# Differential attention with routed experts on one core: experts' steps spread by TensorE columns, and the two attentions of half the head groups added on VectorE

## The chip, the cores and the metric

The kernel runs on one core of a Trainium2 chip. The core has a matrix engine (TensorE, PE in the profile, with its weight loads as PEld), VectorE (DVE), ScalarE (ACT), GpSimd (POOL) and SyncE (SP), which only issues transfers. Each engine works through its own queue in order and waits on semaphores. The metric is the device time of one execution in microseconds; lower is better.

## The reference

The input x is (8, 512, 128): eight sequences of 512 tokens. All data are 32-bit floats.

```python
s1, s2 = q·k1 * SCALE, q·k2 * SCALE          # 16 heads of 8, causal
attn = softmax(s1) - sigmoid(lambda) * softmax(s2)
attn = attn / maximum(sum(abs(attn)), 1e-6)
x = layernorm(x + (attn @ v) @ Wo.T)
xn = layernorm(x) * gamma + beta             # router and experts
probs = softmax(xn @ router.T / 1.5); w, idx = top_k(probs, 2)
y = sum over the two chosen of w * (silu(xn @ W1[e]) @ W2[e])     # 8 experts, 128 -> 512 -> 128
out = layernorm(x + y)
```

## The kernel before

**Units, slots, rounds.** The attention goes through a sequence in 16 row blocks of Q = 32 queries, each a `Unit` with L = 32, 64, ..., 512 keys. The four heads of a group times 32 queries fill the 128 partitions; there are NG = 4 groups. Four units make a token block of 128 tokens (32 blocks in all, n = 0 to 31). A unit with L up to 256 is early: two slots, each with two groups and both softmaxes. A later unit has four slots, each with two groups and one softmax. One call of `round_of` (line 1062) issues one round; a sequence has 16 early and 32 late rounds.

**Order in a round.** `round_of` writes out the order for every engine by hand. For the current slot (`now`), with the next one as `ahead`: the multiplication by V of units that are through (`times_v`, line 469) and, after every fourth unit, `reciprocals`; the scores of `ahead` on TensorE (line 343, with the causal mask added by line 352) into one of two PSUM buffers of the pool `ps_s`; on ScalarE the copies of the last round's transposes (`evacuate`, lines 457 and 459); the row maxima of `now` on VectorE (lines 365 and 373); the transposes of pieces combined in the round before (line 437); then `combine`; then the exponentials of `now` on ScalarE (line 383), which also add up their rows. After that come one task each of `misc` (projections, the end of a block) and `routing`, one of `moves` or `gathers`, and up to two experts' steps.

**Two softmaxes.** `exps` leaves both exponentials of a group unscaled in `et`, at index 0 and 1. With c2 = lambda * sum0 / sum1 (`ratios`), the difference is et0 - c2 * et1, up to a factor per row. `combine` has VectorE take the row sum of max(c2 * et1, et0) (line 409, into `junk`, the sum into `big`), from which `reciprocals` gets the sum of magnitudes, as 2 * big - (1 + lambda) * sum0. GpSimd multiplies et1 by -c2 (line 419). TensorE transposes both and adds them in PSUM: two matmuls per group and 128 keys.

**Experts.** Tokens are routed in chunks: four sparse ones of 6, 9, 9 and 6 blocks and a last dense one of 2. When a chunk's last block is through, `route_tasks` computes the choice, `send` scatters the rows to DRAM by expert with indirect transfers on GpSimd's queue (line 751), and `go` puts the experts' steps into a queue. A sparse chunk of nb blocks has 2nb + 7 tiles of 128 rows. `hidden` computes a tile's hidden layer (line 874) in a PSUM buffer of the pool `ps_m` (two buffers); `turn` transposes a gathered tile, computes the output of an earlier one (lines 845 and 854) and issues the loads of a later tile's rows and weights (256 KB twice) on SP's queue. `gathers` fetch the results back (line 899) and add them (line 909).

**When a step goes.** `times` estimates each round by its columns, and `go` sets `pace`, experts' steps per unit of that time, up to the next chunk's estimated arrival. Each round adds its time times `pace` to `due`, and a step goes for each whole `due`. After the attention `round_of` runs without `now`, and `due` grows by 2 per round.

Of the kernel before, what the change touches and what calls it, by code (L numbers as in the profile page):

```python
# [9 lines left out]
F32 = mybir.dt.float32  # L10
# [3 lines left out]
AF = mybir.ActivationFunctionType  # L14
ALU = mybir.AluOpType
# [5 lines left out]
def kernel(  # L21
# [16 lines left out]
    P = 128  # L38
# [95 lines left out]
    with ExitStack() as actx:  # L134
# [29 lines left out]
        won = aw.tile([P, D], F32, name="won")  # L164
        wo_sb = aw.tile([P, 4, D], F32, name="wo_sb")
        slam = aw.tile([P, NG], F32, name="slam")
        slam1 = aw.tile([P, NG], F32, name="slam1")
        hm = aw.tile([P, 4], F32, name="hm")
        hms = aw.tile([P, 4], F32, name="hms")
# [1 line left out]
        i4 = aw.tile([P, 4, Q], BF16, name="i4")  # L171
        mk = aw.tile([P, Q], BF16, name="mk")
        junk = aw.tile([P, T], F32, name="junk")

        xts = {}

# [47 lines left out]
            )  # L224
        nc.scalar.activation(slam, slam, AF.Sigmoid)
        nc.vector.tensor_scalar(slam1, slam, 1.0, None, ALU.add)
        for h in range(4):
            nc.vector.tensor_scalar_mul(wo_sb[:, h, :], won, hm[:, h : h + 1])

# [86 lines left out]
        class Unit:  # L316


            def __init__(self, b, j, blk):
# [11 lines left out]
                self.et = ep.tile([P, NG, 2, T], F32, tag="et", name=f"et_{b}_{j}")  # L331
                self.aT = self.c2 = None

            def scores(self, slot):
                gp, s = slot
                qb, kT, _ = qkv[self.b]
                L, j = self.L, self.j
                sc = ps_s.tile([P, 2, T], F32, tag="sc", name=f"sc_{self.b}_{j}_{gp}_{s}")
                for si in range(2) if s is None else (s,):
                    lo = 0 if s is not None else si * (T // 2)  # L340
                    for gi in range(2):
                        r = slice(32 * (2 * gp + gi), 32 * (2 * gp + gi) + 32)
                        nc.tensor.matmul(  # L343
                            sc[:, gi, lo : lo + L],
                            lhsT=qb[r, j].rearrange("p h q -> p (h q)"),
                            rhs=kT[r, si, :L],
                            start=True,
                            stop=False,
                        )
                    for gi in range(2):  # L350
                        r = slice(32 * (2 * gp + gi), 32 * (2 * gp + gi) + 32)
                        nc.tensor.matmul(  # L352
                            sc[:, gi, lo + L - Q : lo + L],
                            lhsT=i4[r].rearrange("p h q -> p (h q)"),
                            rhs=mk[r],
                            start=False,
                            stop=True,
                        )
                return sc
# [31 lines left out]
            def ratios(self):  # L391

                sums, jj = self.blk["sums"], self.jj
                c1 = sp.tile([P, NG], F32, tag="c1", name=f"c1_{self.b}_{self.j}")
                nc.vector.tensor_mul(c1, sums[:, 0, jj, :], slam)
                self.c2 = sp.tile([P, NG], F32, tag="c2", name=f"c2_{self.b}_{self.j}")
                r2 = sp.tile([P, NG], F32, tag="r2", name=f"r2_{self.b}_{self.j}")
                nc.vector.reciprocal(r2, sums[:, 1, jj, :])
                nc.vector.tensor_mul(self.c2, c1, r2)

            def combine(self, piece):

                if self.c2 is None:
                    self.ratios()
                L = self.L
                for g in piece:
                    nc.vector.scalar_tensor_tensor(  # L409
                        junk[:, :L],  # L410
                        self.et[:, g, 1, :L],
                        self.c2[:, g : g + 1],
                        self.et[:, g, 0, :L],
                        ALU.mult,
                        ALU.max,
                        accum_out=self.blk["big"][:, self.jj, g : g + 1],
                    )
                for g in piece:
                    nc.gpsimd.tensor_scalar(  # L419
                        self.et[:, g, 1, :L],  # L420
                        self.et[:, g, 1, :L],
                        self.c2[:, g : g + 1],
                        -1.0,
                        ALU.mult,
                        ALU.mult,
                    )

            def widths(self):
                return [min(P, self.L - P * kb) for kb in range(self.n)]

            def transposes(self, piece):

                pt = ps_t.tile([P, 4, P], F32, tag="pt", name=f"pt_{self.b}_{self.j}_{piece[0]}")
                for x_, g in enumerate(piece):
                    for kb, kw in enumerate(self.widths()):
                        for k in range(2):
                            nc.tensor.matmul(  # L437
                                pt[:kw, x_ * self.n + kb, :],
                                lhsT=self.et[:, g, k, kb * P : kb * P + kw],
                                rhs=ident,  # L440
                                is_transpose=True,
                                start=(k == 0),
                                stop=(k == 1),
                            )
                return pt

# [30 lines left out]
        def block_tasks(b, i, blk):  # L477
# [7 lines left out]
            def reciprocals():  # L485
                s["oraw"] = op.tile([P, JT, P], F32, tag="oraw", name=f"oraw_{n}")
                nc.scalar.copy(s["oraw"], blk["po"])

                dg = bp.tile([P, JT, NG], F32, tag="dg", name=f"dg_{n}")
                nc.vector.tensor_mul(  # L490
                    dg, blk["sums"][:, 0], slam1.unsqueeze(1).to_broadcast([P, JT, NG])
                )
                nc.vector.scalar_tensor_tensor(dg, blk["big"], 2.0, dg, ALU.mult, ALU.subtract)
                nc.vector.scalar_tensor_tensor(
                    dg, blk["sums"][:, 0], 1e-6, dg, ALU.mult, ALU.max
                )
                rd = bp.tile([P, JT, NG], F32, tag="rd", name=f"rd_{n}")
                nc.vector.reciprocal(rd, dg)
                s["rexp"] = op.tile([P, JT, NG, 32], F32, tag="rexp", name=f"rexp_{n}")
                nc.gpsimd.tensor_copy(s["rexp"], rd.unsqueeze(3).to_broadcast([P, JT, NG, 32]))  # L500
# [78 lines left out]
        def route_tasks(ch):  # L579
# [176 lines left out]
                )  # L756

            def go():
                nonlocal pace
                first, *others = sparse_tasks(ch) if ch.sparse else dense_tasks(ch)  # L760

                experts.insert(max(0, len(experts) - 4), first)
                experts.extend(others)

                k = chunks.index(ch) + 1
                later = [at for at in arrival[k:] if now_at + 3 < at < time_all]
                pace = len(experts) / max((later + [time_all])[0] - now_at, 3.0)

            def together(*steps):
                def both():  # L770
# [45 lines left out]
        def silu_doubled(pz, dst, name, pool=hp, tag="th"):  # L816
# [4 lines left out]
                lambda: nc.vector.scalar_tensor_tensor(dst, th, 1.0, pz, ALU.add, ALU.mult)  # L821
            )

        def sparse_tasks(ch):
            n0, nt, nb = ch.n0, ch.nt, ch.nb
            w, xg, xgT, hT = {}, {}, {}, {}
# [42 lines left out]
                    load(t + 2)  # L869

            def hidden(t):
                pz = ps_m.tile([P, NF, P], F32, tag="pm", name=f"pz_{n0}_{t}")
                for f in range(NF):
                    nc.tensor.matmul(  # L874
                        pz[:, f, :],
# [160 lines left out]
                if n == ch.n0 + ch.nb - 1:  # L1036
                    misc.append(lambda: routing.extend(route_tasks(ch)))

        def time_of(width):

            return (0.5 + width / 1024) / 1.5

        def times():

            at, now, ends = [], 0.0, {}
            for n in range(NB):
                for j in range(n % NT * JT, (n % NT + 1) * JT):
                    L = (j + 1) * Q
                    now += 2 * time_of(4 * L) if L <= T // 2 else 4 * time_of(2 * L)
                ends[n] = now  # L1050
            seq = now / B
            for ch in chunks:

                behind = seq * (24 + (2 * ch.nb + 3 if ch.sparse else 0)) / 48
                at.append(ends[ch.n0 + ch.nb - 1] + behind)
            return at, now

        arrival, time_all = times()
        pace = due = now_at = 0.0
        attention_done = False  # L1060

        def round_of(now=None, ahead=None):
# [16 lines left out]
            for _ in range(len(to_transpose)):  # L1079
                v, piece = to_transpose.popleft()  # L1080
                to_evacuate.append((v, piece, v.transposes(piece)))
            run(on_dve)
            left = now["left"] if now else 2
            for _ in range(-(-len(to_combine) // left)):
# [15 lines left out]
                room -= step.__name__ == "counts"  # L1100


            for _ in range(1 if now else 2):
                if moves:
                    moves.popleft()()
                elif gathers and (now or not misc and not routing):
                    gathers.popleft()()
            if now:
                spent = time_of(2 * now["u"].L * (2 if now["slot"][1] is None else 1))
                now_at += spent  # L1110
                due += spent * pace
            else:
                due += 2
            while due >= 1 and experts and room:
# [91 lines left out]
```

## Time and profile before

| | us |
|---|---|
| median of 3 runs | 1259.22 |
| lowest, highest | 1250.06, 1261.92 |
| the profiled execution | 1256.73 |
| its span, first to last instruction | 1255.0 |
| mean granted TensorE clock in the span (1 is full) | 0.937 |
| scores of the attention, first to last | 20.1 to 1129.7 |
| GpSimd's sends (60) and gathers (60), mean of one | 1.10, 1.02 |

Every time below is from one profiled execution. A group of instructions is shown as line, engine, operation, tile written and tiles read, shape and count, then the busy time in us, the mean of one in ns, and the idle time of the engine just before them with what ended it. f32 matmuls of the scores and the experts leave two records each, transposes one. A matmul's duration is a latency; where several follow each other, the time for all of them tells what one costs.

### The profile page before, as it was taken

What the parts mean: (1) busy time and instruction counts of PE and PEld (TensorE: products, weight loads), DVE (VectorE), ACT (ScalarE), POOL (GpSimd) and SP (SyncE); (2) the same over time, 40 slices, a digit from 0 to 9 for tenths busy, and PEclk for the clock granted to TensorE, in tenths of its full rate; (3) what the DMA queues carried; (4) which work ended last, traced back from release to release, by engine and by line L of the source; (5) the groups of instructions that cost most, each with busy time, mean ns of one, the idle gap of its engine ahead of it and who ended that gap; (6) DMA issues with size and microseconds to landing.
All of it is one profiled execution on the core that took longest, in us unless ns stands there. A gap on an engine that the chain in (4) does not pass through costs nothing.

```text
span 1255.0 us, 30588 instructions
## 1 busy us (share of the span) xinstructions
PE 1142.6 (91%) x10538; PEld 840.1 (67%) x10538; DVE 950.3 (76%) x2900; ACT 806.1 (64%) x2912; POOL 503.6 (40%) x867
## 2 busy tenths in 40 slices
PE   4999999889999899999999899998999899997776
PEld 3666666556666776677666776676667677776675
DVE  3588768876788778788689778879778877974656
ACT  3568757666777767777676777776667565763221
POOL 3242334363322333237556332233643652353333
PEclk8599969887999989998999999999999989998998
DMA  8000000011111111101213122121222333434762
GB/s 240 1 2 2 2 9 2 24 40 49 39 45 43 50 43 43 45 27 52 74 40 87 52 62 63 54 64 44 66 82 84 94 89 109 126 91 139 210 185 67
DMA packets 115593, 82.85 MB, mean 66 GB/s; under 512 B 9584, under 2 KB 100976, under 8 KB 115440
## 3 DMA queue, kind: packets, MB, share of 16 engines
q1 hardware_dynamic: 97632, 66.67, 18.5%
q0 software_dynamic: 3840, 7.87, 2.3%
q10 hardware_dynamic: 13968, 6.37, 1.8%
q8 instruction: 84, 1.38, 0.5%
q14 instruction: 69, 0.57, 0.2%
HBM read 63.31 MB, written 17.56 MB: 64 GB/s over the span
## 4 chain that ended last, share of the span: by engine, by line
PE 62%; DVE 16%; ACT 8%; issue 5%; POOL 4%; DMA 3%; ACTq 0%; SPq 0%; POOLq 0%; another core or an unknown queue 0%; DVEq 0%
PE pt L437 21%; PE sc L343 12%; PE sc_None L343 6%; PE po L469 6%; PE pz L874 5%; ACT et L383 5%; PE pa L854 5%; DVE junk L409 3%; DVE nm L373 2%; PE pmo L520 2%; DMA xs<-xh,row 2%; DVE nm L365 2%; ACT aT L457 1%; POOL qb L292 1%; POOL et L419 1%
## 5 line engine op out<-in xcount | busy, mean ns | idle before, releaser
L419 POOL TENSOR_SCALAR et<-et,c 128x224 f32<-128x224 f32 (+15 forms) x512 | 268.1, 529 | 477.2 <-DVE junk L409 336.4
L437 PE MATMUL pt<-ident,et 128*128 128x128 f32 (+3 forms) x2560 | 391.8, 293 | 38.4 <-POOL et L419 18.3
L437 PEld LDWEIGHTS pt<-ident,et 128*128 128x128 f32 (+3 forms) x2560 | 276.6, 137 | 159.7 <-issue 51.6
L383 ACT ACTIVATE et<-sc,nm 128x512 f32<-128x512 f32 (+7 forms) x512 | 299.3, 591 | 56.5 <-DVE nm L373 33.8
L373 DVE TENSOR_REDUCE nm<-sc 128x2 f32<-128x576 f32 (+7 forms) x256 | 251.6, 983 | 43.5 <-PE sc L352 41.8
L409 DVE SCALAR_TENSOR_TENSOR junk<-et,c 128x224 f32<-128x224 f32 (+15 forms) x512 | 264.1, 516 | 9.6
L343 PE MATMUL sc<-kT,qb 32*128 32x384 f32 (+7 forms) x1024 | 242.8, 550 | 7.7 <-ACT et L383 6.8
L457 ACT COPY aT<-pt 128x256 f32<-128x256 f32 (+1 forms) x336 | 149.1, 444 | 141.6 <-PE pt L437 135.1
L383 ACT ACTIVATE et<-sc_None,nm 128x256 f32<-128x256 f32 (+7 forms) x512 | 187.2, 378 | 21.6 <-DVE nm L365 10.9
L343 PE MATMUL sc_None<-kT,qb 32*128 32x128 f32 (+7 forms) x1024 | 139.0, 387 | 17.2 <-ACT et L383 16.7
L365 DVE TENSOR_REDUCE nm<-sc_None 128x4 f32<-128x256 f32 (+7 forms) x128 | 96.1, 751 | 46.7 <-PE sc_None L352 46.4
L343 PEld LDWEIGHTS sc_None<-kT,qb 32*128 32x128 f32 x1024 | 88.0, 213 | 53.4 <-ACT et L383 24.9
L112 POOL TENSOR_TENSOR l_rs<-l_ve,nhalf 128x1 f32<-128x1 f32 x96 | 61.5, 640 | 145.3 <-DVE l_ve L110 110.9
L343 PEld LDWEIGHTS sc<-kT,qb 32*128 32x128 f32 x1024 | 77.4, 184 | 57.2 <-ACT et L383 22.2
L874 PE MATMUL pz<-xgT,w 128*128 128x128 f32 x704 | 99.3, 286 | 12.4 <-DVE xgT L848 11.5
L469 PE MATMUL po<-aT,vt 128*32 128x128 f32 (+3 forms) x2560 | 107.8, 288 | 0.0
L383 ACT ACTIVATION_READ_ACCUMULATOR et<-sc_None,nm 128x1 f32 x512 | 104.0, 203 | 0.0
L383 ACT ACTIVATION_READ_ACCUMULATOR et<-sc,nm 128x1 f32 x512 | 101.9, 199 | 0.0
L874 PEld LDWEIGHTS pz<-xgT,w 128*128 128x128 f32 x704 | 89.5, 199 | 17.7 <-DVE xgT L848 14.0
L854 PE MATMUL pa<-w,hT 128*128 128x128 f32 x704 | 98.2, 285 | 0.6 <-ACT ysb L864 0.6
L854 PEld LDWEIGHTS pa<-w,hT 128*128 128x128 f32 x704 | 91.3, 202 | 1.6 <-issue 0.9
L459 ACT COPY aT<-pt 32x128 f32<-32x128 f32 (+5 forms) x288 | 84.6, 294 | 9.7 <-PE pt L437 9.6
(143 smaller groups left out, 1284.8 us busy)
## 6 DMA issues: line engine op xcount, KB each, us to landing
w<-in_w_dram SPq DMA_DIRECT2D x192, 256.0 KB
xg<-xs SPq DMA_DIRECT2D x88, 64.0 KB
ys<-ysb ACTq DMA_DIRECT2D x88, 64.0 KB
xs<-zero SPq DMA_DIRECT2D x2, 1600.0 KB
xs<-zero SPq DMA_DIRECT2D x2, 1216.0 KB
xt<-in_x_dram SPq DMA_DIRECT2D x8, 256.0 KB
out_dram<-ot SPq DMA_DIRECT2D x32, 64.0 KB
xs<-xh,row POOLq DMA_INDIRECT x60
```

Source lines behind the costliest of these rows:

```text
L343: nc.tensor.matmul(sc[:, gi, lo : lo + L], lhsT=qb[r, j].rearrange("p h q -> p (h q)"), rhs=kT[r, si, :L], start=True, stop=False,)
L365: nc.vector.tensor_reduce(self.nm[:, g, :], sc.rearrange("p g (s l) -> p g s l", s=2)[:, :, :, : self.L], AX.X, ALU.max, negate=True,)
L373: nc.vector.tensor_reduce(self.nm[:, g, s], sc[:, :, : self.L], AX.X, ALU.max, negate=True)
L383: nc.scalar.activation(self.et[:, g, si, : self.L], sc[:, gi, lo : lo + self.L], AF.Exp, bias=self.nm[:, g, si : si + 1], accum_out=self.b ...
L409: nc.vector.scalar_tensor_tensor(junk[:, :L], self.et[:, g, 1, :L], self.c2[:, g : g + 1], self.et[:, g, 0, :L], ALU.mult, ALU.max, accum_ ...
L419: nc.gpsimd.tensor_scalar(self.et[:, g, 1, :L], self.et[:, g, 1, :L], self.c2[:, g : g + 1], -1.0, ALU.mult, ALU.mult,)
L437: nc.tensor.matmul(pt[:kw, x_ * self.n + kb, :], lhsT=self.et[:, g, k, kb * P : kb * P + kw], rhs=ident, is_transpose=True, start=(k == 0) ...
L457: nc.scalar.copy(self.aT[:, g, :full, :], src[:, :, :full, :])
L459: nc.scalar.copy(self.aT[: w[-1], g, full, :], src[: w[-1], :, full, :])
L469: nc.tensor.matmul(self.blk["po"][32 * g : 32 * g + 32, self.jj, :], lhsT=vt[:kw, kb, 32 * g : 32 * g + 32], rhs=self.aT[:kw, g, kb, :], s ...
L854: nc.tensor.matmul(pm[:, 1, :], lhsT=hT[y][:, f, :], rhs=w[y][1][:, f, :], start=(f == 0), stop=(f == NF - 1),)
L874: nc.tensor.matmul(pz[:, f, :], lhsT=w[t][0][:, f * P : (f + 1) * P], rhs=xgT[t], start=True, stop=True,)
```

## The change

From block 10 on, groups 2 and 3 of every unit are handled in another way: VectorE adds the two exponentials itself, into `et` at index 0, with a negated c2 (`slams` holds lambda for groups 0 and 1 and minus lambda for groups 2 and 3). GpSimd's multiplication is left out for them, TensorE transposes one tile in place of two, and ScalarE computes the row sum of magnitudes directly (`magnitudes`, issued after the transposes and ahead of the exponentials of the round). `reciprocals` computes the sum of magnitudes from `big` only for the other groups.

The planner gets a list of rounds with an estimated time t and a number of TensorE columns c for each. `go` looks for a level of columns per us such that the sum of max(0, level * t - c) up to the next chunk's arrival equals 1088 columns per step; each round adds max(0, level * t - c) / 1088 to `due`. In the last sequence two moves or gathers go per round. After the attention, `hidden` of a sparse chunk takes its PSUM buffer from `ps_s`.

```diff
+        nc.vector.tensor_copy(slams[:, 0:2], slam[:, 0:2])
+        nc.vector.tensor_scalar_mul(slams[:, 2:4], slam[:, 2:4], -1.0)
...
+                self.added = range(NG) if b * NT + j // JT < 10 else range(2)
...
-                nc.vector.tensor_mul(c1, sums[:, 0, jj, :], slam)
+                nc.vector.tensor_mul(c1, sums[:, 0, jj, :], slam if len(self.added) == NG else slams)
...
                 for g in piece:
+                    added = g in self.added
                     nc.vector.scalar_tensor_tensor(
-                        junk[:, :L],
+                        junk[:, :L] if added else self.et[:, g, 0, :L],
                         self.et[:, g, 1, :L],
                         self.c2[:, g : g + 1],
                         self.et[:, g, 0, :L],
                         ALU.mult,
-                        ALU.max,
-                        accum_out=self.blk["big"][:, self.jj, g : g + 1],
+                        ALU.max if added else ALU.add,
+                        **({"accum_out": self.blk["big"][:, self.jj, g : g + 1]} if added else {}),
                     )
                 for g in piece:
+                    if g not in self.added:
+                        continue
                     nc.gpsimd.tensor_scalar(
...
+            def magnitudes(self, piece):
+
+                for g in piece:
+                    if g not in self.added:
+                        nc.scalar.activation(
+                            junka[:, : self.L],
+                            self.et[:, g, 0, : self.L],
+                            AF.Abs,
+                            accum_out=self.blk["big"][:, self.jj, g : g + 1],
+                        )
...
-                        for k in range(2):
+                        sets = 2 if g in self.added else 1
+                        for k in range(sets):
                             nc.tensor.matmul(
...
-                                stop=(k == 1),
+                                stop=(k == sets - 1),
...
-                pace = len(experts) / max((later + [time_all])[0] - now_at, 3.0)
+                later = [at for at in arrival[k:] if now_at + 4 < at < len(rounds)]
+                stretch = rounds[now_at : (later + [len(rounds)])[0]]
+                low, high = 0.0, 1e5
+                for _ in range(50):
+                    level = (low + high) / 2
+                    if sum(max(0.0, level * t - c) for t, c in stretch) < STEP * len(experts):
+                        low = level
+                    else:
+                        high = level
...
+        def hidden_bank():
+            return ps_s if attention_done else ps_m
...
+        STEP = 1088.0
...
+                if L <= T // 2:
+                    rounds += [(1.8 + 1.57e-3 * 4 * L, 7.0 * L)] * 2
+                else:
+                    rounds += [(1.1 + 1.57e-3 * 2 * L, 3.5 * L)] * 4
+                at_end[b * NT + j // JT] = len(rounds)
+
+        arrival = [
+            at_end[ch.n0 + ch.nb - 1] + 16 + (8 + 2 * ch.nb + 3 if ch.sparse else 0) for ch in chunks
+        ]
...
                 to_evacuate.append((v, piece, v.transposes(piece)))
+                v.magnitudes(piece)
...
-            for _ in range(1 if now else 2):
+            for _ in range(1 if now and now["u"].b < B - 1 else 2):
...
-                due += spent * pace
+                t, c = rounds[now_at]
+                now_at += 1
+                due += max(0.0, level * t - c) / STEP
```

## What the change was predicted to do

> **What bounds the kernel now.** First the page: the engines' busy times, and the row of the granted clock.
>
> ```profile
> PE 1142.6 (91%) x10538; PEld 840.1 (67%) x10538; DVE 950.3 (76%) x2900; ACT 806.1 (64%) x2912; POOL 503.6 (40%) x867
> ...
> PEclk8599969887999989998999999999999989998998
> ```
>
> TensorE is nearly always busy, and its clock is full but for single slices, most of them in the first half. The costliest groups that the change touches come next:
>
> ```profile
> L419 POOL TENSOR_SCALAR et<-et,c 128x224 f32<-128x224 f32 (+15 forms) x512 | 268.1, 529 | 477.2 <-DVE junk L409 336.4
> L437 PE MATMUL pt<-ident,et 128*128 128x128 f32 (+3 forms) x2560 | 391.8, 293 | 38.4 <-POOL et L419 18.3
> ...
> L383 ACT ACTIVATE et<-sc,nm 128x512 f32<-128x512 f32 (+7 forms) x512 | 299.3, 591 | 56.5 <-DVE nm L373 33.8
> ```
>
> The mean of 293 ns for a transpose is a latency. In the chain of waits cut to 637–646 us, six of them take 0.81 us, 0.13 us each, and it shows what a late round (one scores step of a row block with over 256 keys) is made of:
>
> ```profile
> 639.06 0.95 PE sc L343 x4
> 640.01 0.02 PE sc L352 x2
> 640.02 0.81 PE pt L437 x6
> ```
>
> Scores and transposes follow each other with no gap: TensorE sets the round, 1.77 us here, plus one step times V per four rounds (0.79 us for 24). In the timeline of the same place ScalarE has two exponentials of 0.60 us and copies of about 0.5 us, 1.7 us of that 1.77, so it is nearly as full. Then the window sums by stretch; I cut where the scores of a sequence begin (32 keys) and where they pass 256. Columns: stretch, its us, busy us (and instructions) of PE, PEld, DVE, ACT, POOL, granted clock, DMA.
>
> ```profile
> 270.00:324.00 54.00, 48.28 (x441) 36.44 (x442) 34.70 (x129) 32.65 (x151) 20.61 (x40) 0.75 0.15 44
> ...
> 408.00:459.00 51.00, 47.30 (x488) 37.09 (x486) 35.83 (x133) 34.94 (x155) 17.71 (x36) 0.87 0.15 44
> 459.00:543.00 84.00, 82.64 (x760) 57.08 (x759) 69.51 (x184) 62.27 (x203) 26.77 (x44) 1.00 0.17 48
> ...
> 681.00:729.00 48.00, 42.84 (x503) 34.81 (x501) 38.79 (x143) 35.63 (x159) 18.32 (x37) 1.00 0.22 62
> ```
>
> Late stretch (third line): TensorE 98% busy at full clock, VectorE 83%, ScalarE 74%. Early stretches (the others): TensorE is less bound, and the clock is down to 0.75 where few experts' steps run.
>
> **Steps of experts, counted.** The planner is arithmetic on counts, so its order can be worked out from the code, before and after. Experts' steps (hidden, turn, loads) per sequence 2 to 7, early/late: before 4/12, 5/12, 5/15, 7/16, 7/22, 14/34; after 8/4, 12/4, 11/9, 15/10, 15/16, 20/35. The trace agrees for before: 48 and 64 matmul records of pz (8 a step) in late stretches 3 and 5 are 6 and 8 hidden steps. So 33 steps leave the late stretches, 39 come into early ones, and the rounds after the attention fall from 40 to 37. The last sparse chunk starts 8 rounds sooner, because sends go two per round in the last sequence.
>
> **A. Transposes and magnitudes.** 22 blocks, 2 groups, 4 row blocks, 1 to 4 key tiles: 456 transposes fewer, of which 6 x 56 = 336 in late stretches. At 0.13 us that is 44 us late and about 14 us early, the bound if TensorE stayed alone. ScalarE gets 176 magnitudes. No such operation is in the trace; the copies from `pt` cost 0.37 us for 256 elements and 0.59 us for 512, so 0.16 us + 0.83 ns per element: 0.49 us at the late mean of 400, 0.28 us at the early mean of 144. The upper bound is an exponential with its own read of the sum, 0.59 + 0.20 us. That is 96 x 0.49 + 80 x 0.28 = 69 us more on ScalarE. GpSimd loses 176 x 0.53 us, which were idle cover: it waits for VectorE 336 us. VectorE loses the accumulator read (0.08 us x 176 = 14 us); the combine itself keeps its length.
>
> A late unit with three key tiles, without experts: TensorE 4 x 1.77 + 0.95 = 8.0 us, after the change 8.0 - 6 x 0.13 = 7.2. ScalarE 4 x 1.7 = 6.8, after it + 2 x 0.48 = 7.8. The bound passes to ScalarE, and the unit gains 0.3 us, not 0.8. With four tiles: TensorE 4 x 2.02 + 1.14 = 9.2, after it 8.2; ScalarE about 7.9 (exponentials 1.3, copies 0.7), after it 9.0. So again 0.2 to 0.5. Eight units make about 3 us per late stretch, six stretches **-18 us**. Early: up to 14 us off TensorE against 22 us on ScalarE, where neither is full (42.8 and 35.6 of 48): **0**. GpSimd's step leaves the path of half the groups, at most half of the 18.3 us that TensorE waited for it; I keep it for the range.
>
> The Trainium skill speaks on one danger here ("ScalarE: Activation LUTs", Table sets): a function outside the loaded set costs a table load, about 2.7 us, but abs is in every set. The trace has two table loads, 1.28 us each, both before 21 us; were abs to swap tables, two loads for each of 176 magnitudes would be 450 us by that row. I take none.
>
> **B. The spreading.** A step in a late round is 8 matmuls, 0.89 us in the chain near 1090 us; TensorE is bound, so 33 x 0.89 = 29 us leave. In early rounds of sequences 5 and 6 (full clock) the starts of the scores lie 2.5 to 3.1 us apart without a step and 2.9 to 3.5 with one: some 0.7 us a step, 39 x 0.7 = 27 us come back. VectorE hides none of it, it is at 38.8 of 48. A step brings the rest of its work along: per pair tanh 0.60 and a copy 0.27 us on ScalarE, 0.68 and 0.41 us on VectorE, three loads on SP's queue, a store on ScalarE's (0.33 us). With 15 steps sequence 5 early holds 35.6 + 4.5 + 3.5 = 44 us of ScalarE and 38.8 + 4.4 - 1.3 = 42 us of VectorE in about 53; the loads double a DMA share of 0.22. None of these becomes the bound, so the 0.7 us stands. Net **-2**. What remains is the clock. Sequence 2 early took 54.1 us with 4 steps at 0.75, sequence 3 51.0 with 5 at 0.87, sequence 5 48.4 with 7 at 1.00. Levelled by 0.7 per step the first two are 7.8 and 4.0 us too long. With 8 and 12 steps they should run as sequence 5 does, but steps begin only a few rounds into sequence 2: **-8**, of at most 12.
>
> "TensorE: Matmul & The Clock Gate" (Part 1) says that the clock is either full or half, by how busy the array was in the last 3.4 us. By that rule 0.75 of 54 us and 0.87 of 51 us are 27 + 13 us at half clock, and TensorE's work would shrink by 20 us where the rows give 12; VectorE's share of the early rounds explains why the rows give less.
>
> **C. The last sequence.** Two sends per round queue on GpSimd, and a send waits for the landing of the one before it; each line is its start, its length and the idle time ahead of it:
>
> ```profile
> 1115.30 0.65 POOL L419 TENSOR_SCALAR et<-et,c 128x448 f32<-128x448 f32 x1
> 1116.80 1.34 POOL L751 DMA_INDIRECT xs<-xh,row  x1 [0.85 <-DMA xs<-xh,row]
> 1118.18 0.64 POOL L419 TENSOR_SCALAR et<-et,c 128x448 f32<-128x448 f32 x1
> 1119.68 1.05 POOL L751 DMA_INDIRECT xs<-xh,row  x1 [0.85 <-DMA xs<-xh,row]
> ```
>
> The least spacing in the trace is 2.6 us. One send fits a round of about 3.2 us, two do not. Twelve in six rounds take 31 us against 19. Behind them on GpSimd stand the scalings of groups 0 and 1 (TensorE's transposes wait for these), then the spread of the reciprocals, which TensorE's normalise step needs in the same round. Ten sends stand ahead of it, done at 24.5 us + 0.6, and TensorE gets there at about 5 x 3.2 + 1.7 = 17.6 us: **+7**. In return three rounds after the attention go; that part takes 125 us for 40 rounds, 3.1 each: **-9**. Gathers, too, go two per round early in sequence 7: 2 x 1.02 us on GpSimd in rounds of 4 us, hidden.
>
> **D. The hidden layers' bank.** After the attention `pz` takes the scores' banks. What TensorE waits in the whole trace for a bank of `pm` is 5.6 us before the turn (released by hT on VectorE); the chain there is turn, copy, scale, hidden in series, which no bank changes. **-3**, between 0 and -6. The tiny operations on 128x16 tiles per block stay as many as they were: 0.
>
> Sum: -18 + 0 - 2 - 8 + 7 - 9 - 3 = -33 us. The profiled execution took 1256.7 us, 2.5 us under the median, so 1256.7 - 33 + 2.5 = **1226 us**.
>
> **Rivals.** *1. ScalarE's queue (slower).* The magnitudes stand ahead of the round's exponentials in an in-order queue. If a late round then waits for scores, maxima, magnitude and exponentials in series, the magnitudes add themselves and the shorter transposes free nothing. For it: ScalarE at 1.7 of 1.77 us. Against it: two buffers of scores, and 135 us over all in which ScalarE waited for transposes, some of which the magnitudes would fill. Half of the 69 us exposed gives -33 + 18 + 35 = +20: 1279. It decides once 15 of the 69 us, a fifth, are exposed. Chance 0.20.
>
> *2. TensorE stays the bound.* ScalarE's waits absorb the magnitudes, and the whole 44 us late and half of 14 early are kept: -33 - 26 - 7 = -66, 1193. For it: 26% of the late stretch is idle on ScalarE. Against: the sum by units above. Chance 0.13.
>
> *3. It does not do what it says.* The planner evens a TensorE that is no longer the bound; the late stretches gain nothing from A, steps cost early what they cost late and the clock stays low (the loads and first steps come too late), and the sends eat the tail's three rounds: between -10 and 0, about 1255. Chance 0.15.
>
> **Numbers.** The forecast keeps 0.52. Three runs of before lie 12 us apart; about 1% can be told from no change. Faster by over 1% (under 1246.6): nearly all of the forecast and of rival 2, a little of 3: 0.65. Within 1%: most of 3, edges of the forecast and of 1: 0.15. Slower: 0.20. The range runs from rival 2 with its best case cut (1195) to the near part of rival 1 (1268). The forecast's own is 1208 to 1242: A between -30 and -5, C between -8 and +5.
>
> **What would show it.** Late stretches of sequences 3 to 6 some 8 to 10 us shorter each with ScalarE at 90%, early ones 1 to 6 us longer, granted clock near 1.00 early in sequences 2 and 3; GpSimd waiting on sends about 31 us in the last sequence, and TensorE waiting there for the reciprocals' spread. Rival 1 would show as VectorE and TensorE idle until `et L383`; rival 2 as TensorE still 97% busy late. I am wrong if the magnitude takes 0.8 us, if a step costs nothing early, or if the clock falls in late rounds emptied of steps.

## The result and the profile after

Median 1310.87 us (1302.35 to 1315.07, four runs) against 1256.77 us of the kernel before in the same comparison: ratio 1.0425, 95% interval 1.0349 to 1.0501. The change makes the kernel 4% slower; 1226 us was forecast, with a range up to 1268.

The page of the changed kernel (1302.35 us, span 1300.7): busy times, granted clock, and the groups that answer to those of before.

```profile
PE 1135.2 (87%) x10082; PEld 819.0 (63%) x10082; DVE 942.5 (72%) x2726; ACT 867.0 (67%) x3264; POOL 405.9 (31%) x691
...
PEclk8599969897999798988969898999979889969898
...
L459 PE MATMUL pt<-ident,et 128*128 128x128 f32 (+3 forms) x2104 | 350.4, 304 | 39.1 <-POOL et L429 16.6
...
L389 ACT ACTIVATE et<-sc,nm 128x512 f32<-128x512 f32 (+7 forms) x512 | 298.1, 589 | 40.0 <-DVE nm L379 32.7
...
L349 PE MATMUL sc<-kT,qb 32*128 32x384 f32 (+7 forms) x1024 | 255.2, 576 | 38.9 <-ACT et L389 38.4
```

The 456 transposes are gone, and ScalarE has 61 us more, close to the 69 of the prediction. Two rows are new in kind. TensorE sits idle 38.9 us before the late scores, waiting for the exponentials (the page of before has 7.7 us there). And the clock falls to 7 and 6 in slices after the first third, where before it hardly left 9; its mean is 0.899 against 0.937. The window sums by stretch, with the same columns as before: early sequence 2, early and late 3, early 5.

```profile
269.00:322.00 53.00, 48.12 (x476) 37.07 (x473) 37.48 (x134) 33.94 (x153) 19.19 (x39) 0.84 0.24 68
403.00:462.00 59.00, 51.12 (x505) 40.94 (x503) 37.09 (x125) 42.14 (x194) 10.17 (x21) 0.86 0.22 63
462.00:546.00 84.00, 76.26 (x657) 48.37 (x659) 66.29 (x159) 65.47 (x231) 17.27 (x27) 0.94 0.09 24
698.00:757.00 59.00, 51.04 (x530) 42.06 (x528) 40.45 (x135) 43.65 (x197) 11.06 (x22) 0.91 0.30 85
```

Sequence 2 has no additions in its early rounds and is 1 us shorter; sequences 3 and 5, which have them, are 8 and 11 us longer. The late stretch of sequence 3 takes what it took before, 84 us, with 8 steps and 48 transposes less on TensorE. Over sequences 3 to 6 the early stretches grow by 38 us and the late ones shrink by 3; sequence 7 grows by 24 us; the part after the attention is 8.4 us shorter (116.3).

### The profile page after: what moved, and what is told of

It is laid out like the page before. It is cut to its first block, busy times and chain, and to the rows that moved or that the text cites. A ratio compares the mean times of both kernels' runs of the same rounds, so it can differ in the third digit from the quotient of the medians.

```text
span 1300.7 us, 29678 instructions
## 1 busy us (share of the span) xinstructions
PE 1135.2 (87%) x10082; PEld 819.0 (63%) x10082; DVE 942.5 (72%) x2726; ACT 867.0 (67%) x3264; POOL 405.9 (31%) x691
## 4 chain that ended last, share of the span: by engine, by line
PE 52%; DVE 19%; ACT 14%; issue 6%; POOL 4%; DMA 4%; ACTq 0%; SPq 0%; POOLq 0%; DVEq 0%
PE pt L459 16%; PE sc L349 11%; ACT et L389 8%; PE sc_None L349 5%; PE po L491 5%; PE pa L896 4%; PE pz L916 4%; DVE nm L379 3%; ACT junka L442 2%; DVE junk L417 2%; PE pmo L547 2%; DMA xs<-xh,row 2%; DVE hT L856 2%; DVE nm L371 1%; ACT aT L479 1%
## 5 line engine op out<-in xcount | busy, mean ns | idle before, releaser
L459 PE MATMUL pt<-ident,et 128*128 128x128 f32 (+3 forms) x2104 | 350.4, 304 | 39.1 <-POOL et L429 16.6
L459 PEld LDWEIGHTS pt<-ident,et 128*128 128x128 f32 (+3 forms) x2104 | 234.6, 142 | 162.4 <-issue 50.7
L429 POOL TENSOR_SCALAR et<-et,c 128x64 f32<-128x64 f32 (+15 forms) x336 | 174.0, 523 | 482.9 <-DVE junk L417 378.5
L349 PE MATMUL sc<-kT,qb 32*128 32x384 f32 (+7 forms) x1024 | 255.2, 576 | 38.9 <-ACT et L389 38.4
L417 DVE SCALAR_TENSOR_TENSOR junk<-et,c 128x64 f32<-128x64 f32 (+15 forms) x336 | 171.8, 511 | 8.0
L491 PE MATMUL po<-aT,vt 128*32 128x128 f32 (+3 forms) x2560 | 113.5, 300 | 0.0
L916 PE MATMUL pz<-xgT,w 128*128 128x128 f32 x704 | 106.2, 300 | 6.2 <-DVE xgT L890 3.5
L896 PE MATMUL pa<-w,hT 128*128 128x128 f32 x704 | 102.0, 293 | 7.5 <-DVE hT L856 4.7
L916 PEld LDWEIGHTS pz<-xgT,w 128*128 128x128 f32 x704 | 97.7, 215 | 8.2 <-DVE xgT L890 3.9
L896 PEld LDWEIGHTS pa<-w,hT 128*128 128x128 f32 x704 | 95.0, 210 | 9.9 <-DVE hT L856 7.2
```

The costliest lines, as they stand in the source:

```text
L349: nc.tensor.matmul(sc[:, gi, lo : lo + L], lhsT=qb[r, j].rearrange("p h q -> p (h q)"), rhs=kT[r, si, :L], start=True, stop=False,)
L417: nc.vector.scalar_tensor_tensor(junk[:, :L] if added else self.et[:, g, 0, :L], self.et[:, g, 1, :L], self.c2[:, g : g + 1], self.et[:, g ...
L429: nc.gpsimd.tensor_scalar(self.et[:, g, 1, :L], self.et[:, g, 1, :L], self.c2[:, g : g + 1], -1.0, ALU.mult, ALU.mult,)
L459: nc.tensor.matmul(pt[:kw, x_ * self.n + kb, :], lhsT=self.et[:, g, k, kb * P : kb * P + kw], rhs=ident, is_transpose=True, start=(k == 0) ...
L491: nc.tensor.matmul(self.blk["po"][32 * g : 32 * g + 32, self.jj, :], lhsT=vt[:kw, kb, 32 * g : 32 * g + 32], rhs=self.aT[:kw, g, kb, :], s ...
L896: nc.tensor.matmul(pm[:, 1, :], lhsT=hT[y][:, f, :], rhs=w[y][1][:, f, :], start=(f == 0), stop=(f == NF - 1),)
```

## The experiments

Each time is a median with the ratio to the kernel before on the same chip and its 95% interval. Microseconds gained or lost are the ratio less 1, times 1257; clocks and stretches are those of the profiled execution. "Early 3" is the early stretch of sequence 3. Three theories stood at the start: the magnitudes in ScalarE's queue (S, the first rival of the prediction), the price of a step in an early round, and the clock.

**The four parts alone.** `e1_adds` holds only the changes to `Unit`, `reciprocals` and the call of `magnitudes`; `e2_level` only `rounds`, `arrival`, `go` and `due`; `e4_bank` only `hidden_bank` and `hidden_tag`; and `e3_moves` only this:

```diff
-            for _ in range(1 if now else 2):
+            for _ in range(1 if now and now["u"].b < B - 1 else 2):
```

> Kernel before with the additions of groups 2 and 3 alone (blocks from 10 on; planner, moves and banks as before). The prediction's term A says -18 us (ratio 0.986). Theory 1, ScalarE's queue (the magnitudes stand ahead of the exponentials and are exposed): +25 to +45 us, ratio 1.02 to 1.035, with the early stretches of sequences 3 to 6 some 4 to 6 us longer. Theory 2, the spreading is what costs: -20 to 0 us. Theory 3, only both together cost (late rounds emptied of steps and of transposes let the clock fall): within 10 us of before, clock still 0.93 or more.

> Kernel before with the new planner alone (rounds, level, columns; 4 softmax groups as before, one move per round, banks as before). The prediction's term B says -10 us (0.992). Theory 1 (ScalarE's queue): -10 to 0 us. Theory 2 (a step in an early round costs more than the 0.89 us it frees in a late one): +25 to +45 us, ratio 1.02 to 1.035, the early stretches of sequences 3 to 6 each 6 to 10 us longer, late ones 4 to 7 shorter. Theory 3: within 10 us of before.

> Kernel before with two moves or gathers per round in the last sequence alone; rounds after the attention fall from 40 to 39. The prediction's term C, +7 for the sends and -9 for the tail, here -3 for one round: +4 us (1.003). All three theories: between -5 and +10 us; a rest of more than 15 us would make the last sequence a cause of its own (after the change its two stretches are 24 us longer than before).

> Kernel before with the hidden layers' PSUM buffer taken from the scores' pool after the attention, alone. The prediction's term D: -3 us (0.998), between 0 and -6. All three theories agree; the stretch after the attention, 124.7 us before and 116.3 after the change, would be 119 to 124.

| | median us | ratio | us |
|---|---|---|---|
| e1_adds | 1320.16 | 1.0526 (1.0455 to 1.0598) | +66 |
| e2_level | 1258.54 | 1.0032 (0.9990 to 1.0073) | +4 |
| e3_moves | 1281.10 | 1.0203 (1.0115 to 1.0292) | +26 |
| e4_bank | 1249.15 | 0.9942 (0.9901 to 0.9982) | -7 |

The additions are the loss, more than Theory 1 allowed (+45), the doubled moves a second one. Theory 2 falls: steps spread alone cost nothing that can be told. They do not gain either. Late 4, with 2 hidden layers in place of 5, is the one late stretch that grows; before, then in `e2_level`:

```profile
592.00:681.00 89.00, 84.17 (x753) 56.50 (x753) 73.82 (x205) 61.13 (x201) 50.20 (x68) 0.98 0.23 64
581.00:674.00 93.00, 85.96 (x693) 54.92 (x690) 71.80 (x199) 58.63 (x194) 50.98 (x68) 0.87 0.16 46
```

TensorE has 60 instructions less there, the clock is lower, and the stretch is longer. Windows of `e1_adds`, late 3, early and late 4 (early 4 before: 48.7 us at 0.93):

```profile
466.00:561.00 95.00, 87.49 (x715) 58.81 (x713) 70.87 (x170) 68.65 (x235) 16.96 (x27) 0.89 0.16 43
561.00:622.00 61.00, 55.08 (x463) 42.98 (x462) 39.87 (x145) 40.42 (x187) 21.81 (x32) 0.66 0.10 29
622.00:723.00 101.00, 91.06 (x699) 58.20 (x699) 74.52 (x188) 67.14 (x230) 41.09 (x52) 0.85 0.20 56
```

Late 3 is 11 us longer than before with all steps where they were, and the clock is 0.89 in place of 1.00. The mean over the span is 0.877. The trace's clock records know only 1 and 0.5, so the share at half clock is twice what is missing: 2 x (1 - 0.877) x 1318.8 = 324 us, against 2 x (1 - 0.937) x 1255 = 158 us before.

**Work, place and presence of the magnitudes.** Three variants of `e1_adds`. In `e5_dup` the added tile is transposed twice, the second over the first; in `e6_nomag` the magnitudes are left out; in `e7_maglate` they are issued behind the exponentials of the round:

```diff
-                        for k in range(sets):
+                        for k in range(2):            # e5: lhsT index min(k, sets - 1), start each time
...
-                v.magnitudes(piece)
+                        nc.vector.memset(blk["big"], 1.0)     # e6: once per block from block 10
...
-                v.magnitudes(piece)
+                late.append((v, piece))               # e7: run after exps(now)
```

> The additions alone (1320 us, clock 0.877), but TensorE transposes the added tile twice, the second time over the first, so that its work is as before while ScalarE keeps the magnitudes. Theory G1 (the clock falls because TensorE has less to do): the clock returns to 0.92 or more and the time to 1250 to 1275 us, so that more work makes the kernel faster. Theory S (the magnitudes on ScalarE, ahead of the exponentials, lengthen the rounds by themselves): 1315 to 1350 us, clock below 0.90. The prediction's term A holds no clock at all: by it 1320 us plus some part of 44 us.

> The additions alone, with the magnitudes left out: the row sums of groups 2 and 3 are set to 1 by VectorE, so the output is not the reference's; half the transposes stay gone. Theory S: 1200 to 1260 us, as ScalarE's part is gone. Theory G1 (too little work on TensorE by itself): still 1290 us or more, clock below 0.90. Theory G2 (the clock falls where TensorE idles behind ScalarE, and the transposes matter only together with the magnitudes): 1200 to 1245 us with the clock at 0.93 or more.

> The additions alone, with the magnitudes issued behind the round's exponentials in place of ahead of them; the work of every engine is the same. If their place in ScalarE's queue is what counts (Theory S, my first rival): 1250 to 1285 us. Theory G1: 1305 to 1325 us, unchanged.

Measured, with the clock of the profiled execution: `e5_dup` 1295.55 us, 1.0311 (1.0268 to 1.0354), clock 0.917; `e6_nomag` 1271.12 us, 1.0063 (1.0016 to 1.0110), clock 0.885; `e7_maglate` 1291.82 us, 1.0267 (1.0195 to 1.0340), clock 0.879. No single theory holds, and all three times lie outside the ranges of the theories. The place in the queue is worth 33 us (`e1` minus `e7`, at the same clock, 0.877 and 0.879), needless work on TensorE gains 27 us (`e1` minus `e5`), and without any magnitudes the halved transposes still gain nothing at all.

What the place does can be read in the timeline of the changed kernel (start and length in us, then engine, line, operation):

```profile
485.54 0.52 ACT L389 ACTIVATE et<-sc,nm 128x320 f32<-128x320 f32 x1
...
486.04 0.38 ACT L479 COPY aT<-pt 128x256 f32<-128x256 f32 x1
...
486.20 0.86 PE L349 MATMUL sc<-kT,qb 32*128 32x352 f32 x4 [0.40 <-ACT et L389]
486.29 0.25 ACT L481 COPY aT<-pt 32x128 f32<-32x128 f32 x1
486.44 0.44 ACT L442 ACTIVATE junka<-et 128x288 f32<-128x288 f32 x1
...
486.88 0.53 ACT L389 ACTIVATE et<-sc,nm 128x352 f32<-128x352 f32 x1
```

ScalarE runs without a gap; TensorE waits 0.40 us for the exponentials that free a buffer of scores, and the magnitude (0.44 us from its start to theirs) stands ahead of the next exponentials, which free the next one. Behind the exponentials it has only the copies of the next round behind it. The idle time before the late scores goes from 35.5 us in `e1_adds` to 19.5 in `e7_maglate`:

```profile
L348 PE MATMUL sc<-kT,qb 32*128 32x384 f32 (+7 forms) x1024 | 256.3, 578 | 35.5 <-ACT et L388 34.9
L348 PE MATMUL sc<-kT,qb 32*128 32x384 f32 (+7 forms) x1024 | 245.4, 556 | 19.5 <-ACT et L388 19.1
```

**Both undone, and the halved transposes by themselves.** `e13_maglate_dup` joins e5 and e7; `e14_nomag_dup` joins e5 and e6.

> The additions alone, magnitudes behind the exponentials, and the added tile transposed twice. If the two causes are separate they add: 1320 - 28 - 25 = 1267 us, clock 0.92 or more. If both act through the same thing (TensorE idles, the clock falls): 1285 to 1295 us, no better than either alone.

> The additions without the magnitudes (row sums of groups 2 and 3 set to 1, so the output is not the reference's), and the added tile transposed twice: TensorE's work as before, ScalarE's too, GpSimd's and the accumulator reads less. If halving the transposes gains nothing because the clock falls: 1245 to 1262 us at 0.92 or more, that is below the 1271 us with half the transposes. If the halved transposes do gain and something else in the additions costs: 1285 us or more.

`e13_maglate_dup`: 1266.06 us, 1.0052 (1.0014 to 1.0089), clock 0.934. The two add up: 60 of the 66 us are gone, 33 + 27 apart. `e14_nomag_dup`: 1253.62 us, 0.9954 (0.9918 to 0.9990), clock 0.940. It does 456 needless transposes more than `e6_nomag` and is 14 us faster (0.9954 against 1.0063). Over all their runs the clocks do not overlap: 0.883 to 0.903 in nine of `e6_nomag`, 0.926 to 0.942 in ten of `e14_nomag_dup`. Early and late 3 of `e6_nomag`, then of `e14_nomag_dup`:

```profile
404.00:465.00 61.00, 58.20 (x457) 45.06 (x456) 34.66 (x119) 35.08 (x156) 10.60 (x21) 0.61 0.13 37
465.00:547.00 82.00, 78.60 (x720) 52.65 (x721) 69.92 (x173) 61.67 (x204) 16.95 (x27) 1.00 0.18 50
```

```profile
406.00:452.00 46.00, 41.66 (x493) 33.48 (x493) 34.82 (x121) 35.02 (x158) 10.65 (x21) 1.00 0.17 49
452.00:536.00 84.00, 82.64 (x759) 57.15 (x760) 69.32 (x169) 62.45 (x203) 17.04 (x27) 1.00 0.17 48
```

The late stretch gains 2 us from half the transposes. The early one loses 15: with 32 transposes fewer the clock is 0.61, and TensorE's busy time is 58 us in place of 42. One early stretch proves little: equal instructions took 49.8 us at 0.80 and, in `e13_maglate_dup`, 45.4 at 0.89 (early 1). The verdict rests on the times of the whole kernel. Added up over sequences 2 to 7, one profiled execution each, the stretches say which cause acts where (each is cut where its scores begin; all in us):

| | magnitudes | added tile transposed | early, sum | late, sum | of these at half clock |
|---|---|---|---|---|---|
| before | none | (both tiles) | 311.8 | 549.0 | 61, 10 |
| e1_adds | ahead | once | 343.8 | 583.9 | 143, 99 |
| e5_dup | ahead | twice | 336.5 | 569.4 | 106, 34 |
| e7_maglate | behind | once | 350.4 | 546.4 | 177, 41 |
| e13_maglate_dup | behind | twice | 319.8 | 551.7 | 72, 14 |
| e6_nomag | none | once | 338.8 | 541.3 | 164, 41 |
| e14_nomag_dup | none | twice | 305.8 | 551.7 | 51, 20 |

The place of the magnitudes acts in late stretches (583.9 to 546.4) and, with the tile transposed twice, in both (18 us late, 17 early). With them behind or left out, halving the transposes saves 5 to 10 us late and costs 31 to 33 early, where the time at half clock grows by over 100 us. With them ahead it costs both, 15 us late and 7 early. The magnitudes themselves, behind the exponentials and with the tile transposed twice, cost 12 us by the whole times (`e13` minus `e14`), by the sums all of it early. Undone in this order, the 66 us are 33 for the place, 27 for the halved transposes beside the magnitudes (14 without them), 12 for the magnitudes, less 6 that the rest of the additions gains (`e14`).

**Late units alone.** `e10_late` is `e7_maglate` with the additions for units over 256 keys only:

```diff
+                self.added = range(NG) if b * NT + j // JT < 10 or self.early else range(2)
```

> Additions in the late units alone (over 256 keys, from block 10 on), magnitudes behind the exponentials, everything else as before. If the loss sits in the early rounds (their clock, and 0.36 us per magnitude): late stretches 0 to 4 us shorter each, early ones as before, 1235 to 1258 us. If the late rounds lose clock by themselves: 1270 us or more. The prediction's own arithmetic for the late stretches, -3 us each, gives 1240 us.

1280.05 us, 1.0196 (1.0128 to 1.0264). The time is that of the second answer, but not by its reason: the late stretches of sequences 3 to 7 are as long as before within 4 us, but the early ones, whose own units are handled as before (only the end of the last late unit falls into them, with 16 transposes less and 8 magnitudes), take 56, 62, 54, 55 and 61 us against 51, 49, 48, 47 and 63, at clocks of 0.64 to 0.92. Why a late stretch with less work leaves a colder early one (a lower clock) behind was not settled.

**Matmuls for the clock's sake.** `e11_warm` is the kernel before with needless work in early rounds; `e15_bankwarm1` has one such matmul and the bank of `e4_bank`.

```diff
+                if self.early and self.b:
+                    for x_ in range(4):               # e15: range(1)
+                        nc.tensor.matmul(pt[:, x_, :], lhsT=ident, rhs=ident, start=True, stop=True)
```

> Kernel before with four needless 128x128 matmuls (the identity by itself, into the transposes' buffer before its use) in every early round of sequences 1 to 7, 0.9 us of TensorE at full clock each. If the clock in early rounds follows how much TensorE does: granted clock early in sequences 1 to 3 from 0.75-0.87 to 0.95 or more, these stretches no longer than before (0 to -6 us each), those of 4 to 7 some 5 to 10 longer, since a step there costs 0.7 us: 1255 to 1290 us. If the clock does not follow the work: every early stretch 10 to 14 us longer, 1320 us or more, clock under 0.93.

> Kernel before with the hidden layers' bank and one needless 128x128 matmul of the identity per early round of sequences 1 to 7 (0.22 us each, 25 us of TensorE in all; four of them held the clock at 1.00 and cost 39 us). If one suffices to hold the clock: early stretches of sequences 1 to 3 at 0.95 or more and 3 to 5 us shorter each, 1235 to 1250 us. If not: 1255 to 1275 us, clock as before.

`e11_warm`: 1296.49 us, 1.0319 (1.0259 to 1.0379), clock 0.966. `e15_bankwarm1`: 1253.18 us, 0.9940 (0.9903 to 0.9977), clock 0.965. Both times lie a few us above the ranges they were expected in. Early 1 of `e11_warm`, then of `e15_bankwarm1` (before: 49.8 us at 0.80):

```profile
137.00:186.00 49.00, 46.77 (x534) 38.91 (x533) 33.53 (x128) 32.46 (x150) 17.62 (x36) 1.00 0.03 7
```

```profile
137.00:179.00 42.00, 38.84 (x459) 30.84 (x459) 32.36 (x127) 32.20 (x150) 17.18 (x36) 1.00 0.03 8
```

In this stretch the clock follows the work. One matmul per round, expected at 0.22 us at full clock, leaves it 3 to 7 us shorter than the two times above without one; four make it as long as before. All three kernels with such matmuls (`e16_fixwarm`, below, too) hold 1.00 here, and none of the others does (0.76 to 0.89). It is not so everywhere: early 2 stands at 0.89 in `e15_bankwarm1`, and in `e11_warm`, with four, at 0.80 and 61.1 us, longer than before (54.1 us at 0.75). In the kernel's time `e15_bankwarm1` cannot be told from the bank alone (0.9942); both are 0.6% faster than the kernel before, and the warming itself is not shown to pay.

**The doubled moves.** `e8_sends2` doubles only the sends in the last sequence.

> Kernel before with two sends per round in the last sequence, gathers one per round as before. With both doubled the time was 1281 us, early stretch of sequence 7 13.5 us longer and late one 11 longer. If the sends are most of it (my prediction's +7, and a longer stall than I counted): the late stretch 8 to 14 us longer, the early one as before, 1262 to 1270 us in all. If the gathers are: within 5 us of before.

1273.51 us, 1.0154 (1.0078 to 1.0229): +19 of the +26, just above the 1262 to 1270 of the first answer. Its late stretch of sequence 7 takes 120.3 us (before 103.3), the early one 59.7 (62.8). The late one before, then in `e8_sends2`:

```profile
1027.00:1130.00 103.00, 99.68 (x918) 76.22 (x919) 85.20 (x248) 69.61 (x220) 41.51 (x58) 0.98 0.38 110
1028.00:1149.00 121.00, 110.70 (x919) 83.53 (x918) 85.68 (x249) 69.94 (x222) 40.87 (x59) 0.89 0.35 100
```

With both doubled (`e3_moves`) the early one takes 76.3 us and the late one 114, so by these profiles the gathers cost in the early one, though by the whole times (+26 and +19, each good to about 10) their share is not sure. GpSimd's timeline in the changed kernel at the sends:

```profile
1138.51 0.96 POOL L778 DMA_INDIRECT xs<-xh,row  x1 [1.91 <-DMA xs<-xh,row]
1141.00 0.96 POOL L778 DMA_INDIRECT xs<-xh,row  x1 [1.53 <-DMA xs<-xh,row]
1143.49 0.96 POOL L778 DMA_INDIRECT xs<-xh,row  x1 [1.53 <-DMA xs<-xh,row]
1144.49 0.61 POOL L429 TENSOR_SCALAR et<-et,c 128x416 f32<-128x416 f32 x1
1145.98 1.05 POOL L778 DMA_INDIRECT xs<-xh,row  x1 [0.88 <-DMA xs<-xh,row]
```

Every send here waits for the landing of the one before, 2.5 us apart, and the scaling that the transposes need comes after a row of them. Twelve took from 1129.5 to 1159.7.

**The change mended.** `e9_maglate1`: the whole change with the magnitudes behind the exponentials and one move per round. `e12_levelbanklate`: the same with additions in late units only. `e16_fixwarm`: `e9_maglate1` with one needless matmul ahead of every piece's transposes from sequence 1 on.

> The whole change with two of its parts turned back: the magnitudes behind the round's exponentials, and one move per round in the last sequence. If the causes found so far add up (28 us for the magnitudes' place, 20 to 27 us for the doubled moves): 1311 - 28 - 25 = 1258 us, no slower than before. If the spreading and the additions have a cost of their own together (early rounds hold both the steps and the magnitudes): 1275 to 1295 us.

> The parts that cost nothing alone, together: the spreading, the hidden layers' bank, additions in late units alone with the magnitudes behind the exponentials; one move per round. Sum of the single results: +4 (spreading) - 7 (bank) - 5 to -15 (late additions): 1238 to 1252 us. If the late rounds, emptied of steps and of transposes, lose the clock: 1265 us or more, late stretches of sequences 2 to 6 below 0.95.

> The change with the magnitudes behind the exponentials and one move per round (1267.5 us), and one needless 128x128 matmul of the identity ahead of every piece's transposes from sequence 1 on (336 of them, 0.22 us each, 74 us of TensorE, about what the halved transposes save). If the rest of its loss is the clock: half-clock time falls from 283 to under 130 us and the time to 1240 to 1260 us. If full matmuls hold the clock no better than transposes do: 1275 us or more.

`e9_maglate1` 1267.52 us, 1.0070 (1.0026 to 1.0114); `e12_levelbanklate` 1264.24 us, 1.0072 (1.0028 to 1.0115); `e16_fixwarm` 1265.18 us, 1.0044 (1.0001 to 1.0087), clock 0.949. Mending the two faults takes the +53 us to +9, between the two answers expected. None of the three beats the kernel before; the additions gain nothing here even without their faults. `e12_levelbanklate` misses its sum (1238 to 1252); as its second answer has it, late 3, 4 and 6 stand at 0.88, 0.78 and 0.87, though its time stays just under the 1265 us named there. `e16_fixwarm` misses its 1240 to 1260: the clock comes back, but its matmuls cost about what that is worth.

## Why the prediction was wrong

**A, transposes and magnitudes: -18 forecast, +66 measured.** This is the step that failed, in both of its halves: late -18 forecast, +35 measured; early 0 forecast, +32 measured (sums of the profiled `e1_adds`). The count of transposes was right, and ScalarE's addition came to 61 us for 69. Two things were left out. First, "the bound passes to ScalarE, and the unit gains 0.3 us" compared sums of work per engine; it left out where in the queue the work stands. Ahead of the exponentials it delays the release of the scores' buffers, 33 us. That was rival 1, at a chance of 0.20, with about this size (half of 69 us exposed). Second, the sum priced TensorE's work at full clock, and put early rounds at nothing because no engine was full there. With less work the clock fell, 27 us of the 66 by `e5_dup`, and `e6_nomag` against `e14_nomag_dup` shows it with no magnitudes in play (14 us). It fell mostly in early rounds, in `e1_adds` as much in late ones. That the clock falls with the transposes is shown by these pairs; by what rule is open. Even without the two faults the late gain was too high: 3 us over the six stretches with the magnitudes behind (`e7_maglate`), 8 with none, for 18. The sum for the unit of three key tiles also counts 0.95 us for the step times V where the prediction's own reading has 0.79; with 0.79 that unit gains 0.1 us, not 0.3.

**B, the spreading: -10 forecast, +4 measured (-1 to +9).** The early half came out: in `e2_level` the early stretches of sequences 2 to 7 are 18 us longer together, where +27 for steps and -8 for the clock were counted; early 2 and 3 take 52.8 and 51.0 us with 4 and 7 steps more than in their 54.1 and 51.0 before. The late half failed: 16 us shorter in place of 29. The time at half clock there rises from 10 to 44 us (early it falls from 61 to 31), most plainly in late 4, 0.87 where 0.98 stood. That is the sign the prediction named, "the clock falls in late rounds emptied of steps", and late 4 shows it in each kernel with the spreading (0.77 to 0.87; without it 0.91 to 1.00, but for 0.85 in `e1_adds`). These are single profiled executions, and the whole of B cannot be told from nothing. In the whole change the spreading does help the additions: the four parts alone sum to +89, together they give +53. The doubled moves are not the reason: `e7_maglate`, the spreading and the bank alone sum to +30, and together (`e9_maglate1`) they give +9. The mean clock, 0.877 with the additions alone and 0.899 in the whole, speaks for warmer early rounds; that was not tested apart.

**C, the last sequence: -2 forecast, +26 measured alone.** The mechanism of the sends was right, its size not: 19 us for 7. I counted the wait of the reciprocals' spread once and nothing for the clock, which is 0.89 in that stretch of `e8_sends2` (before 0.98). "Gathers ... hidden" was wrong in the early stretch. And no gain shows from the three rounds fewer after the attention: with the bank alone that part takes 115.0 us in 40 rounds, in the whole change 116.3 in 37.

**D, the bank: -3 forecast, -7 measured (-12 to -2).** The forecast lies inside the interval. The part after the attention is 9.7 us shorter, 124.7 to 115.0, and over all profiled kernels it takes 120 to 126 us without the bank and 113 to 119 with it. Before, with its wait ahead of the hidden layers, then `e4_bank`:

```profile
1130.00:1255.00 125.00, 90.81 (x662) 81.27 (x658) 70.08 (x208) 31.35 (x65) 44.67 (x55) 0.91 0.53 150
PE pz L874 <- DVE xgT L848: 11.3, 11, 1.9
1137.00:1252.00 115.00, 84.97 (x658) 76.95 (x658) 69.68 (x208) 31.17 (x63) 44.60 (x55) 0.94 0.57 164
```

With the bank that wait has no row; TensorE's weight loads wait 0.2 us there (before 13.4). "The chain there is turn, copy, scale, hidden in series, which no bank changes" missed that hidden layers can begin earlier with buffers of their own.

The times of rival 2 (TensorE stays the bound) and rival 3 (no effect) are excluded by the interval, though two signs of rival 3 came: the late stretches gained little from A, and the sends ate the rounds of the tail.

The Trainium skill, "TensorE: Matmul & The Clock Gate" (Part 1), says that the clock is full or half by how busy the array has been. The records here show only these two values; that the profile's busy time decides between them they do not show (58.2 of 61 us at 0.61 in early 3 of `e6_nomag`). Its Part 4 says that transposes do not count as busy in the same way. Here 456 needless transposes raise the mean clock from 0.885 to 0.940 and shorten the kernel, so the measurement decides: in this kernel they help to hold the clock.

## What to carry to other kernels

Before work is taken from the busiest engine, look whether its clock is already dropping somewhere; if so, less work can come back as slower work, and a run that does the removed work needlessly tells the two apart. When work moves to an engine with idle time, the sum of busy times does not decide: ask which instruction is queued behind it, and what that one releases. Where a transfer waits for the one before it (here 2.5 us each), issuing two per round only moves the wait ahead of everything else in that queue.

## What was not expected of the hardware

A busy TensorE does not keep its clock. In early 3 of `e6_nomag` TensorE is busy 58.2 of 61 us, and in no place of that stretch or the two after it are PE and PEld both idle for more than 1.01 us, yet the mean clock is 0.61. Part of that busy time is the slow clock itself: in `e14_nomag_dup`, with 32 more transposes, it is 41.7 of 46 us at 1.00. Every spell between two changes in the clock records lasts a whole multiple of 3.41 us, and one at half clock can be long: 41.0 us in early 3 and 54.6 us in early 4 of `e6_nomag`. With all transposes early 3 stood at 0.87 to 1.00 (before, `e4_bank`, `e13`, `e14`; 0.79 in `e5_dup`), so a part of the difference is from one execution to the next. One 128x128 matmul of f32 per round of 3 us was enough to lift early 1 from 0.80 or 0.89 to 1.00.
